# Layer 1 of a two-layer row attention: the softmax sums inverted once each and spread by transfers, and the seven block products added up on the way out of PSUM

## The chip, the cores and the metric

The kernel runs on one core of a Trainium2 chip. The metric is the time of one execution on the device in microseconds; the figure for a version is the median of its runs. TensorE is called PE, its weight load PEld, VectorE DVE, ScalarE ACT, GpSimd POOL, and SyncE, which issues the transfers, SP.

## The reference, cut to what matters

Two residual layers work on x of shape (1, 128, 256, 256): 128 rows of 256 tokens with 256 channels. Each begins with a group norm. Layer 0 is a gated attention with 8 heads and a pair bias; the change does not touch its arithmetic. Layer 1 is banded attention with 4 heads of 64 channels, in which a token sees the tokens up to 16 places away:

```
xn  = group_norm(x)
q, k, v = split(xn @ w_in.T + b_in)
s   = where(|i - j| <= 16, q k^T / sqrt(64), -inf)      per row and head
a   = softmax(s) v
out = x + a @ w_out.T + b_out
```

Everything is fp32.

## The kernel before, in words

Layer 0 walks through the 128 rows and leaves its output in DRAM as x1, channels on the partitions. Layer 1 reads that back in pairs of rows (`load1`, tile yg) and works in *rounds* of two rows. The order of the instructions on PE, ACT, DVE and POOL is the order of the program text, since `tc.manual_schedule` is on for these engines. SP is not in that list before; the scheduler places its transfers.

A round i, with s = 2i, runs these steps:

- `normal(i+2)` normalizes the pair i+2 on ACT (four activations, tile 1xn) and lets POOL make its four sums and differences (`row_sums`, tile 1ts).
- `scores(s)` and `scores(s+1)`: PE multiplies q and k in blocks of 64 keys by 96 queries, ACT takes the exponentials (1ex), POOL multiplies by the band's mask (1p) and adds two halves to 1zp, from which the softmax sums come.
- `attend(s-2)` and `attend(s-1)`: PE multiplies the weights 1p with the values into one half of the PSUM tile avz, and 1zp with a block of ones into the other half. The ones have 64 columns, so each softmax sum stands on the 64 partitions of its head, ready for a division by element.
- `total`: ACT copies the sums to SBUF (1z) and adds them up for a check at the end. `inverse`: DVE takes the reciprocal of 128x512 sums for each row. `divide`: DVE multiplies av by it, into 1at.
- `finish(i-3)`: DVE adds bias and residual to the output of pair i-3, turns it (`turn`, four transposes of 32x32 blocks) and stores it (`store`, four transfers of 128 KB).
- `row_sums` of 1at on DVE (tile 1att), `least` (DVE, minimum of the sums, for the check).
- `stretch(i+1, i-2)`: the three projections of 256 by 256 for a pair: q and k of pair i+1 and the output projection o of pair i-2.
- `values(s+2)` and `values(s+3)`: PE makes v in 64 matmuls (p1v), ACT copies it out.

A projection of a pair is done with seven products of 128x128 blocks in place of eight (class `Seven`). Each of the streams q, k and o has one PSUM bank with two halves. Product 2 goes to the upper half and is taken out at once[...]. Then the products follow each other into the two halves and accumulate there; after some of them ACT copies a half out (`take`). In the version before, all copies of the three streams are on ACT, and POOL adds the copies to the results afterwards (`add_two`, `add_mid`). `in_turn` issues the products of the three streams interleaved: 2 for each, (1, 5) for each, (3, 6) for each, 7 for each, 4 for each.

[...] Four form a ring (`proj_bank`, `sim_bank`) that scores, products and values use one after the other; four hold two avz tiles.

After the last round the two remaining pairs go through a tail without seven products (`project`, `add`, `turn_row`), and the check reads zmin and zsum; only if it fails, a slower path runs.

Of the kernel before, what the change touches and what calls it, by code (L numbers as in the profile page):

```python
# [9 lines left out]
F32 = mybir.dt.float32  # L10
AF = mybir.ActivationFunctionType
ALU = mybir.AluOpType
# [3 lines left out]
P = 128  # L16
# [23 lines left out]
def conv_preact_kernel(  # L40
# [142 lines left out]
    zmin = const.tile([P, 2 * S], F32, name="zmin")  # L183
    zsum = const.tile([P, 2 * S], F32, name="zsum")
# [387 lines left out]
    class Seven:  # L572


        def __init__(self, pool, weights, x, t, name, tag, by_token=False, bias=None, mid="mid"):
            self.weights, self.x, self.t, self.by_token, self.bias = weights, x, t, by_token, bias
            self.name, self.tag = name, tag
            self.to = pool.tile([P, 4, R], F32, tag=tag, name=name, bufs=2 if mid == "mid" else 1)

            self.mid = pool.tile([P, 2, R], F32, tag=mid, name=f"mid{name}", bufs=2 if mid == "mid" else 1)  # L580
# [19 lines left out]
        def copy(self, to, ps, half):  # L600

            if self.bias is None:
                nc.scalar.copy(to, ps)
            else:
                nc.scalar.activation(to, ps, AF.Identity, bias=self.bias[:, half : half + 1])

        def take(self, what):
            if what == "2":
                self.copy(self.two, self.ps[:, 1, :], 0)
            elif what == "15":  # L610
                nc.scalar.copy(self.to[:, 0:4:3, :], self.ps)
            elif what == "6":
                self.copy(self.mid[:, 0, :], self.ps[:, 0, :], 0)
            elif what == "7":
                self.copy(self.mid[:, 1, :], self.ps[:, 0, :], 1)
            elif self.bias is None:
                nc.scalar.copy(self.to[:, 1:3, :], self.ps)
            else:
                self.copy(self.to[:, 1, :], self.ps[:, 0, :], 1)
                nc.scalar.copy(self.to[:, 2, :], self.ps[:, 1, :])  # L620
# [39 lines left out]
    def in_turn(pool, sevens):  # L660

        for p in sevens:
            p.open()
            p.two = pool.tile([P, R], F32, tag=f"two{p.tag}", name=f"two{p.name}", bufs=1)

            p.product(2, p.ps[:, 1, :], first=True)
            p.take("2")
        for p in sevens:
            p.product(1)
            p.product(5)  # L670
            p.take("15")
        for p in sevens:
            p.product(3)
            p.product(6)
            p.take("6")
        for n, what in ((7, "7"), (4, "34")):
            for p in sevens:
                p.product(n)
                p.take(what)
        for p in sevens:  # L680
            p.add_two(p.two)
        for p in sevens:
            p.add_mid()
# [22 lines left out]
    with ExitStack() as both:  # L706
# [6 lines left out]
        ygs = {}  # L713

# [238 lines left out]
        with ExitStack() as lay:  # L953
# [6 lines left out]
            xns, tss, res = {}, {}, {}  # L960
# [30 lines left out]
            def stretch(i, j):  # L991


                streams = [
                    Seven(row, quarters1[w], xns[i], tss[i], f"1{w}{i}", w, bias=bqk[:, 0:2] if w == "q" else None,
                          mid=f"mid{w}")
                    for w in "qk"
                ]
                f, g = streams
                if j >= 0:  # L1000
                    outputs[j] = Seven(row, quarters1["o"], ats[j], ats_t[j], f"1o{j}", "out", mid="mido")
                    streams.append(outputs[j])
                in_turn(row, streams)
                for r in range(2):
                    st[2 * i + r].update(q=f.to[:, 2 * r : 2 * r + 2, :], k=g.to[:, 2 * r : 2 * r + 2, :])
# [50 lines left out]
            def attend(s):  # L1056
                if s < 0:
                    return
                (p, zp), v = hd.pop(s), st[s]["v"]

                avz = ps_av.tile([P, 2, 2, R], F32, tag="avz", name=f"1avz{s}", bufs=2)
                for b in range(NB):
                    for half in range(2):
                        for j in range(2):
                            keys, cols = slice(KB * half, KB * (half + 1)), slice(D1 * j, D1 * (j + 1))
                            q0, p0 = QLO[b], R * (b % 2) + QLO[b]

                            nc.tensor.matmul(
                                avz[cols, half, 0, q0 + QIN[b].start : q0 + QIN[b].stop],
                                lhsT=v[keys, b, cols],  # L1070
                                rhs=p[keys, j, p0 + QIN[b].start : p0 + QIN[b].stop],
                                start=(b == 0), stop=False,
                                skip_group_check=True,
                            )
                for half in range(2):
                    for j in range(2):
                        keys, cols = slice(KB * half, KB * (half + 1)), slice(D1 * j, D1 * (j + 1))
                        nc.tensor.matmul(
                            avz[cols, half, 1, :], lhsT=ones[keys, :], rhs=zp[keys, j, :],
                            start=False, stop=True,  # L1080
                            skip_group_check=True,
                        )
                hd[s] = avz

            def total(s):
                if s < 0:
                    return
                z = att.tile([P, 2, R], F32, tag="z", name=f"1z{s}", bufs=4)
                n = S + s
                nc.scalar.activation(z, hd[s][:, :, 1, :], AF.Identity, accum_out=zsum[:, n : n + 1])  # L1090
                st[s]["z"] = z

            def inverse(s):
                if s >= 0:
                    st[s]["rz"] = att.tile([P, 2, R], F32, tag="rz", name=f"1rz{s}")
                    nc.vector.reciprocal(st[s]["rz"], st[s]["z"])  # L1096

            def divide(s):
                if s < 0:
                    return  # L1100
                i, r = divmod(s, 2)
                if r == 0:
                    ats[i] = row.tile([P, 4, R], F32, tag="at", name=f"1at{i}", bufs=2)
                at = ats[i][:, 2 * r : 2 * r + 2, :]
                nc.vector.tensor_tensor(at, hd.pop(s)[:, :, 0, :], st[s]["rz"], ALU.mult)
                st[s]["at"] = at

            def least(s):
                if s >= 0:
                    n = S + s  # L1110
                    nc.vector.tensor_reduce(zmin[:, n : n + 1], st[s]["z"], axis=AX.XY, op=ALU.min)
# [43 lines left out]
            def finish(i):  # L1155
# [3 lines left out]
                ot = row.tile([P, 4, R], F32, tag="ot2", name=f"1ot2_{i}", bufs=1)  # L1159
                for half in range(2):  # L1160
                    nc.vector.scalar_tensor_tensor(
                        ot[:, half::2, :], outputs[i].to[:, half::2, :], bo_v[:, half : half + 1], ygs[i][:, :, half, :],
                        op0=ALU.add, op1=ALU.add,
                    )
                outputs.pop(i)
                for r in range(2):
                    st[2 * i + r]["ot"] = ot[:, 2 * r : 2 * r + 2, :]
# [5 lines left out]
            with tc.manual_schedule(engines={  # L1173
                mybir.EngineType.PE, mybir.EngineType.Activation, mybir.EngineType.DVE, mybir.EngineType.Pool
# [9 lines left out]
                for s in range(0, S + 2, 2):  # L1184
                    i = s // 2
                    bulk = s < S - 2
                    if bulk:
                        normal(i + 2, True)
                    if s < S:
                        scores(s)  # L1190
                        scores(s + 1)
                    attend(s - 2)
                    attend(s - 1)
                    total(s - 2)
                    total(s - 1)
                    if s < S:
                        finish(i - 3)
                    for r in (s - 2, s - 1):
                        inverse(r)
                        divide(r)  # L1200
                    if bulk:
                        if 0 <= i - 1 < S // 2 - 3:
                            ats_t[i - 1] = row.tile([P, 4, R], F32, tag="att", name=f"1att{i - 1}", bufs=2)
                            row_sums(ats_t[i - 1], ats[i - 1], nc.vector)
                        least(s - 2)
                        least(s - 1)
                        stretch(i + 1, i - 2)
                        values(s + 2)
                        values(s + 3)
                    else:  # L1210

# [3 lines left out]
                        add(s - 4, False)  # L1215
                        add(s - 3, False)
                for s in (S - 2, S - 1):
                    for _ in project(s):
                        pass
                add(S - 2, False)  # L1220
# [6 lines left out]

                for s in (S - 6, S - 5):
                    turn_row(s)
                add(S - 1, True)  # L1230
                for s in (S - 2, S - 4, S - 3):
                    turn_row(s)
                store(S - 1)
                for s in range(S - 4, S):
                    least(s)
# [198 lines left out]
```

## Time and profile before

| | |
|---|---|
| median of 3 runs | 3229.56 us (3226.58 to 3230.96) |
| profiled execution, time | 3227.81 us |
| profiled execution, span of the core | 3226.1 us |
| instructions | 87360 |
| busy over the span | PE 97%, PEld 75%, DVE 91%, ACT 65%, POOL 58% |
| granted TensorE clock, mean | 0.991 |
| layer 1 | from about 2086 us to the end |
| one round of layer 1 | 17.37 us |

The span lies within the execution's own time, which is what the medians count. "Busy" is recorded time in instructions. In a view of waits each line names an engine and line that stood still, and after the arrow the engine and line that ended the wait, then the time in total, how often, and the longest. In a timeline the first two numbers are start and duration in us; "x7" is how many instructions were merged; brackets hold the idle time before. In groups of instructions the last parts are busy time in us, mean ns of one, and idle time before. An fp32 product on PE is recorded as two matmuls.

### The profile page before, as it was taken

Reading aid. Unit: us, or ns where it says so; the run is one execution under the profiler, and the core shown is the slowest. Engines: PE = TensorE matmul, PEld = TensorE weight load, DVE = VectorE, ACT = ScalarE, POOL = GpSimd, SP = SyncE. Lnnn points to the kernel's source line nnn. Section 1 sums busy time; section 2 is a strip of 40 time slices with the busy share of each in tenths; the row PEclk is TensorE's granted clock in tenths of the full one; section 3 lists DMA queues with packets and bytes.
Section 4 is the critical chain, followed back from the end, with each engine's and each line's share of the span. In section 5 each row is a group of like instructions: output and inputs, shape, how many; then the busy total and the mean of one; then the engine's idle time right before and its main releaser. Section 6 shows DMA issues by size and latency. Waiting matters only on the chain.

```text
span 3226.1 us, 87360 instructions
## 1 busy us (share of the span) xinstructions
PE 3117.8 (97%) x36843; PEld 2435.0 (75%) x36843; DVE 2938.5 (91%) x3629; ACT 2105.2 (65%) x4621; POOL 1876.1 (58%) x1780
## 2 busy tenths in 40 slices
PE   7889999999999999999999999999999999999997
PEld 4567777777777777777777777678888888888886
DVE  4669999999999999999999999869999999999998
ACT  4656666666666666666666666477777777777774
POOL 3034444444444444444444444288999999999996
PEclk9989999999999999999999999999999999999998
DMA  9931111111111111111111111012222222222222
GB/s 382 423 93 46 54 41 40 41 34 38 36 41 34 40 34 41 34 41 34 41 34 41 34 41 34 28 28 67 55 67 56 66 67 54 67 67 54 67 59 44
DMA packets 346191, 209.40 MB, mean 65 GB/s; under 512 B 273592, under 2 KB 339136, under 8 KB 339648
## 3 DMA queue, kind: packets, MB, share of 16 engines
q1 hardware_dynamic: 344896, 201.37, 21.8%
q8 instruction: 292, 4.78, 0.6%
q0 software_dynamic: 752, 2.36, 0.2%
q14 instruction: 107, 0.88, 0.1%
q10 hardware_dynamic: 144, 0.00, 0.0%
HBM read 136.59 MB, written 67.11 MB: 63 GB/s over the span
## 4 chain that ended last, share of the span: by engine, by line
PE 82%; ACT 9%; DMA 5%; issue 2%; DVE 2%; POOL 0%; SPq 0%; DVEq 0%; ACTq 0%; POOLq 0%
PE sim L766 8%; PE p1v L1015 7%; PE po L691 7%; PE av L798 7%; PE bv L798 7%; PE p1q L594 6%; PE pv L598 6%; PE pq L594 6%; PE pk L594 5%; PE p1k L594 5%; PE pg L594 5%; PE p1o L594 5%; DMA pr<-in_L_conv_pair_repr_dram 4%; PE zs L812 4%; ACT 1ex L1044 3%; ACT 1xn L975 3%
## 5 line engine op out<-in xcount | busy, mean ns | idle before, releaser
L779 ACT ACTIVATE ex<-sim 128x512 f32<-128x512 f32 x1024 | 548.1, 606 | 431.5 <-PE sim L766 431.5
L788 DVE TENSOR_TENSOR both<-ex 128x512 f32<-128x512 f32 x512 | 483.7, 983 | 75.2 <-ACT ex L779 74.5
L1096 DVE RECIPROCAL 1rz<-1z 128x512 f32<-128x512 f32 x128 | 426.0, 3328 | 39.0 <-ACT 1z L1090 39.0
L828 DVE RECIPROCAL d<-d 128x512 f32<-128x512 f32 x128 | 429.2, 3353 | 4.4
L623 POOL TENSOR_TENSOR v<-v,twovg 128x256 f32<-128x256 f32 x64 | 75.0, 1173 | 548.3 <-ACT twovg L642 548.3
L766 PE MATMUL sim<-q,k 32*128 32x256 f32 x4096 | 295.7, 401 | 1.1 <-ACT ex L779 1.1
L691 PE MATMUL po<-at,out_sb 128*128 128x256 f32 x1024 | 285.1, 382 | 4.0 <-DVE at L846 4.0
L766 PEld LDWEIGHTS sim<-q,k 32*128 32x128 f32 x4096 | 186.4, 184 | 102.7 <-issue 95.1
L798 PE MATMUL bv<-bias_sb,v 128*32 128x256 f32 x4096 | 244.5, 379 | 0.7 <-DVE t L843 0.7
L798 PE MATMUL av<-ex,v 128*32 128x256 f32 x4096 | 244.5, 379 | 0.0
L1015 PEld LDWEIGHTS p1v<-w_in_t,1xn 128*64 128x64 f32 x4096 | 222.3, 137 | 21.6 <-PE p1k L594 20.2
L1015 PE MATMUL p1v<-w_in_t,1xn 128*64 128x128 f32 x4096 | 237.7, 274 | 0.3 <-DVE 1xn L977 0.3
L1046 POOL TENSOR_TENSOR 1p<-1ex,seen 128x768 f32<-128x768 f32 x128 | 232.5, 1817 | 2.6 <-ACT 1ex L1044 2.6
L623 POOL TENSOR_TENSOR q<-q,twoqk 128x256 f32<-128x256 f32 x64 | 47.3, 740 | 296.7 <-ACT twoqk L642 296.7
L691 PEld LDWEIGHTS po<-at,out_sb 128*128 128x128 f32 x1024 | 185.8, 192 | 25.3 <-issue 4.3
L798 PEld LDWEIGHTS bv<-bias_sb,v 128*32 128x32 f32 x4096 | 133.1, 110 | 88.8 <-issue 1.1
L798 PEld LDWEIGHTS av<-ex,v 128*32 128x32 f32 x4096 | 133.2, 110 | 87.8 <-issue 0.3
L748 DVE TENSOR_SCALAR xn<-xt,mean,rstd 128x256 f32<-128x256 f32 x256 | 180.0, 742 | 0.0
L1022 ACT COPY 1v<-p1v 128x512 f32<-128x512 f32 x128 | 75.0, 586 | 145.0 <-PE p1v L1015 145.0
L1053 POOL TENSOR_TENSOR 1zp<-1p 128x512 f32<-128x512 f32 x128 | 162.7, 1271 | 10.0
L333 DVE BATCH_NORM_STATS2 stats<-xs 128x6 f32<-128x128 f32 x512 | 100.3, 276 | 63.9 <-DMA xs<-in_x_dram 63.9
L827 DVE SCALAR_TENSOR_TENSOR d<-g,z 128x512 f32<-128x512 f32 x128 | 113.1, 884 | 40.7 <-ACT z L825 40.5
(290 smaller groups left out, 8541.0 us busy)
## 6 DMA issues: line engine op xcount, KB each, us to landing
pr<-in_L_conv_pair_repr_dram SPq DMA_DIRECT2D x32, 1024.0 KB, 23.1
xs<-in_x_dram SPq DMA_DIRECT2D x16, 2048.0 KB, 23.3
x<-o SPq DMA_DIRECT2D x64, 512.0 KB, 3.0
yg<-x SPq DMA_DIRECT2D x64, 512.0 KB, 3.9
out_dram<-1o SPq DMA_DIRECT2D x256, 128.0 KB, 3.4
xg<-in_x_dram SPq DMA_DIRECT2D x252, 128.0 KB, 3.1
qkv_sb<-in_L_conv_qkv_proj_dram POOLq DMA_DIRECT2D x4, 192.0 KB, 12.7
w_raw<-in_L_conv_w_in_dram POOLq DMA_DIRECT2D x1, 768.0 KB, 13.4
```

The source lines that it names most:

```text
L594: nc.tensor.matmul(out, lhsT=weights, rhs=moving, start=first, **flags)
L598: nc.tensor.matmul(out[:, cols], lhsT=moving[:, cols], rhs=weights, start=first and t2 == 0, **flags)
L691: nc.tensor.matmul(ps[:, m, :], lhsT=w[:, kt, m * P : (m + 1) * P], rhs=at[:, kt, :], start=(kt == 0), stop=(kt == 1),)
L748: nc.vector.tensor_scalar(xns[i][:, 2 * r + half, :], xt[:, half, :], mean0[:, half : half + 1], rstd0[:, half : half + 1], op0=ALU.subtra ...
L766: nc.tensor.matmul(sims[j][:, kt, :], lhsT=k[p0 : p0 + D0, 2 * r + half, kt * P : (kt + 1) * P], rhs=q[p0 : p0 + D0, 2 * r + half, :], sta ...
L779: nc.scalar.activation(ex[:, j], sims[j], AF.Exp, scale=1.0 / math.sqrt(D0))
L788: nc.vector.tensor_tensor(both[:, j : j + 2], ex[:, j : j + 2, 0, :], ex[:, j : j + 2, 1, :], ALU.add)
L798: nc.tensor.matmul(to[D0 * j : D0 * (j + 1), half, :], lhsT=v[:, 2 * r + half, c0 : c0 + D0], rhs=weights(4 * half + j, kt), start=(kt == ...
L828: nc.vector.reciprocal(d, d)
L1015: nc.tensor.matmul(ps[KB * half : KB * (half + 1), b, :], lhsT=xns[i][:, 2 * r + kt, KB * b : KB * (b + 1)], rhs=w_in_t[:, kt, 2 * C + P * ...
L1046: nc.gpsimd.tensor_tensor(p.rearrange("p j (r c) -> p (j r) c", c=WROW)[:, :, 0 : 2 * WSTEP] .rearrange("p r (t c) -> p r t c", c=WSTEP)[: ...
L1096: nc.vector.reciprocal(st[s]["rz"], st[s]["z"])
```

## The change

The change does four things in layer 1.

1. *The sums.* `attend` handles a pair at once. The av products of both rows go to one PSUM tile, 1av, and the sums to another, 1zs, with one buffer each. The block of ones is replaced by `place`, whose columns are ones for 16 partitions out of 64, so that the sums of both rows stand one beneath the other, 16 partitions each. `inverse` copies one half to SBUF (ACT), adds the other (DVE), takes the reciprocal of 128x256 (DVE), writes one partition of each sixteen to DRAM (rz_far, two transfers of 4 KB), and reads them back spread over 64 partitions each (near, two transfers of 256 KB). `divide` multiplies the whole pair by near. `bounds` does the work of `total` and `least` for the check on a pair.
2. *The products.* Class `Summed` takes every product out as it is made, in the order 2, 1, 5, 6, 7, 4, 3 for each of the three streams. Products 2, 5, 6 and 4 are copied out, for q and k by ACT, for o by DVE with bias and residual added; 1, 7 and 3 are added by DVE to what is there already. POOL's additions are gone, and so is the residual step of `finish`.
3. *Places.* `normal(i+2)` stands after `stretch`, `divide` after that, and the `row_sums` of 1at are on POOL. SP joins the engines whose order is the text's.
4. *The tail* is written for pairs.

The core of the diff:

```diff
-    def in_turn(pool, sevens):
+    class Summed(Seven):
...
+        def out(self, to, half, m, r):
+
+            ps = self.ps[:, half, :]
+            if self.y is not None:
+                nc.vector.scalar_tensor_tensor(
+                    to, ps, self.bias[:, m : m + 1], self.y[:, r, m], op0=ALU.add, op1=ALU.add
+                )
+            elif self.bias is None:
+                nc.scalar.copy(to, ps)
+            else:
+                nc.scalar.activation(to, ps, AF.Identity, bias=self.bias[:, m : m + 1])
+
+        def take(self, n):
+            to, ps = self.to, self.ps
+            if n == 2:
+                self.out(to[:, 0], 1, 0, 0)
+            elif n == 1:
+                nc.vector.tensor_tensor(to[:, 0], ps[:, 0, :], to[:, 0], ALU.add)
+            elif n == 5:
+                self.out(to[:, 3], 1, 1, 1)
+            elif n == 6:
+                self.out(self.mid, 0, 0, 1)
+            elif n == 7:
+                nc.vector.tensor_tensor(to[:, 3], ps[:, 0, :], to[:, 3], ALU.add)
+            elif n == 4:
+                self.out(to[:, 1], 0, 1, 0)
+            elif n == 3:
+                nc.vector.tensor_tensor(to[:, 2], ps[:, 1, :], self.mid, ALU.add)
+
+    def in_turn(sevens):
 
         for p in sevens:
             p.open()
-            p.two = pool.tile([P, R], F32, tag=f"two{p.tag}", name=f"two{p.name}", bufs=1)
 
             p.product(2, p.ps[:, 1, :], first=True)
-            p.take("2")
...
+            p.take(2)
+        for n in (1, 5, 6, 7, 4, 3):
             for p in sevens:
                 p.product(n)
-                p.take(what)
-        for p in sevens:
-            p.add_two(p.two)
-        for p in sevens:
-            p.add_mid()
+                p.take(n)
...
+            place = att.tile([P, 2, D1], F32, name="place", bufs=1)
+            nc.gpsimd.memset(place, 0.0)
+            for half in range(2):
+                for r in range(2):
+                    c = 32 * half + 16 * r
+                    nc.gpsimd.memset(place[KB * half : KB * (half + 1), r, c : c + 16], 1.0)
...
-            def attend(s):
-                if s < 0:
+            def attend(i):
...
+                av = ps_av.tile([P, 2, 2, R], F32, tag="av", name=f"1av{i}", bufs=1)
+                zs = ps_av.tile([P, 2, 2, R], F32, tag="zs", name=f"1zs{i}", bufs=1)
...
                             nc.tensor.matmul(
+                                zs[cols, half, 0, :], lhsT=place[keys, r, :], rhs=zp[keys, j, :],
+                                start=(r == 0), stop=(r == 1),
                                 skip_group_check=True,
                             )
...
+                zs = hd["av", i][1]
+                z = att.tile([P, R], F32, tag="z", name=f"1z{i}")
+                nc.scalar.copy(z, zs[:, 0, 0, :])
+                nc.vector.tensor_tensor(z, zs[:, 1, 0, :], z, ALU.add)
+                rz = att.tile([P, R], F32, tag="rz", name=f"1rz{i}")
+                nc.vector.reciprocal(rz, z)
+                for j in range(2):
+                    nc.sync.dma_start(
+                        out=rz_far[i % 2, j], in_=rz[D1 * j : D1 * (j + 1)].rearrange("(n c) q -> n c q", c=16)[:, 0, :]
+                    )
+                near = att.tile([P, 2, 2, R], F32, tag="near", name=f"1near{i}", bufs=1)
+                for j in range(2):
+                    nc.sync.dma_start(
+                        out=near[D1 * j : D1 * (j + 1)].rearrange("p h r q -> p (h r q)"),
+                        in_=rz_far[i % 2, j].rearrange("n q -> (n q)").partition_broadcast(D1),
+                    )
+                hd["z", i] = (z, near)
+
+            def divide(i):
+                if i < 0:
                     return
...
+                ats[i] = row.tile([P, 4, R], F32, tag="at", name=f"1at{i}", bufs=2)
+                nc.vector.tensor_tensor(
+                    ats[i].rearrange("p (r h) q -> p h r q", h=2), hd.pop(("av", i))[0], hd["z", i][1], ALU.mult
+                )
...
-                mybir.EngineType.PE, mybir.EngineType.Activation, mybir.EngineType.DVE, mybir.EngineType.Pool
+                mybir.EngineType.PE, mybir.EngineType.Activation, mybir.EngineType.DVE, mybir.EngineType.Pool,
+                mybir.EngineType.SP,
             }):
...
+                for i in range(S // 2):
+                    s = 2 * i
+                    bulk = i < S // 2 - 1
+                    scores(s)
+                    scores(s + 1)
+                    finish(i - 3)
+                    attend(i - 1)
+                    inverse(i - 1)
                     if bulk:
+                        stretch(i + 1, i - 2)
                         normal(i + 2, True)
...
+                        divide(i - 1)
                         if 0 <= i - 1 < S // 2 - 3:
                             ats_t[i - 1] = row.tile([P, 4, R], F32, tag="att", name=f"1att{i - 1}", bufs=2)
-                            row_sums(ats_t[i - 1], ats[i - 1], nc.vector)
...
+                            row_sums(ats_t[i - 1], ats[i - 1], nc.gpsimd)
+                        bounds(i - 1)
                         values(s + 2)
                         values(s + 3)
                     else:
-
                         for r in (s - 4, s - 3):
                             for _ in project(r):
                                 pass
...
+                            add(r, False)
+                        divide(i - 1)
+                last = S // 2 - 1
+                attend(last)
+                inverse(last)
...
+                divide(last)
+                for s in (S - 2, S - 1):
+                    for _ in project(s):
+                        pass
```

## The prediction

> **What bounds the kernel now.** I first read the page's busy shares and slices, to see where the edited stage lies and which engines are full in it.
>
> ```profile
> PE 3117.8 (97%) x36843; PEld 2435.0 (75%) x36843; DVE 2938.5 (91%) x3629; ACT 2105.2 (65%) x4621; POOL 1876.1 (58%) x1780
> ...
> PE   7889999999999999999999999999999999999997
> ...
> DVE  4669999999999999999999999869999999999998
> ...
> POOL 3034444444444444444444444288999999999996
> ```
>
> Layer 1 is the last third (POOL jumps from 4 to 8 or 9). It runs from 2086 us to the end, in 63 rounds of two rows. Next comes the busy time in a stretch well inside it.
>
> ```profile
> 2400.00:2800.00 400.00, 387.44 (x5754) 333.95 (x5753) 393.64 (x369) 289.33 (x691) 369.01 (x324) 1.00 0.25 63
> ```
>
> PE 97%, DVE 98%, POOL 92%: three engines look full, so the shares don't say which sets the round. The view of waits in 2400 to 3100 us (40 rounds) does:
>
> ```profile
> PEld p1q L594 <- ACT two1q L605: 37.9, 40, 1.0
> ...
> PE p1q L594 <- ACT two1q L605: 21.8, 40, 0.6
> PEld p1q L594 <- ACT 1ex L1044: 15.4, 40, 0.4
> ```
>
> PE waits twice in every round, and for ACT only; for DVE and POOL it never waits. PE is the bound, with two short stalls in each round behind ACT. The timeline of one round shows them:
>
> ```profile
> 2705.33 0.60 PE L1078 MATMUL 1avz<-1zp,ones 64*64 64x256 f32 x7
> ...
> 2705.87 0.70 PE L594 MATMUL p1q<-1xn,w_in_t 128*128 128x256 f32 x2
> ...
> 2707.42 0.50 ACT L605 ACTIVATE two1q<-p1q,bqk 128x256 f32<-128x256 f32 x1
> ...
> 2707.97 0.70 PE L594 MATMUL p1q<-1xn,w_in_t 128*128 128x256 f32 x2 [0.54 <-ACT two1q L605]
> ...
> 2708.51 0.59 PE L594 MATMUL p1q<-1ts,sums_1q 128*128 128x256 f32 x2
> ...
> 2708.94 0.59 PE L594 MATMUL p1k<-1xn,w_in_t 128*128 128x256 f32 x2
> ```
>
> Products follow each other every 0.4325 us (2708.51 to 2708.94), recorded 0.59 long, so an end lies 0.16 past the time at which PE is free. The last zs matmul ends at 2705.93, so PE is free at T = 2705.77. The values' first matmul stands at 2715.94 and a round lasts 17.37 us (2698.58 to 2715.94). From T to the values are 10.17 us for 21 products, that is 9.08: **1.09 us of each round are stalls**. Of them 0.21 lie ahead of the first product (ACT does the four 1xn before the exponentials, which free its bank), 0.81 ahead of product 1 of q, 0.07 at the values. A stalled product costs 0.11 beyond its wait, since its weights load unhidden (0.70 against 0.59).
>
> [...] DVE's L568 takes 1.38 us beside POOL's adds and L570 0.41 us alone. [...] the trace has 0.69 at 512, so 0.42 at 256 is my estimate. [...] the trace has no transfer as small as the new ones.
>
> **The change part by part.** *Off DVE:* two reciprocals 128x512, two divides, four subtractions, two reductions, two 1ot:
>
> ```profile
> L1096 DVE RECIPROCAL 1rz<-1z 128x512 f32<-128x512 f32 x81 | 269.2, 3324 | 0.0
> L1161 DVE SCALAR_TENSOR_TENSOR 1ot<-1o,bo_v,yg 128x512 f32<-128x512 f32 x80 | 84.9, 1100 | 0.0
> L569 DVE TENSOR_TENSOR 1att<-1at 128x256 f32<-128x256 f32 x40 | 59.8, 1494 | 0.0
> L1111 DVE TENSOR_REDUCE zmin<-1z 128x1 f32<-128x512 f32 x80 | 50.6, 672 | 0.0
> ```
>
> *On DVE now, per round:* transposes 1.41; the add of z 0.42; one reciprocal of 256 at 6.2 ns per element, 1.75 (0.17 for 2 elements, 3.34 for 512); nine sums out of PSUM at 0.42; four 128x256 out of PSUM with bias and y at 0.46 (L1129: 0.44 and 0.48); one divide of 1024, 1.22; one reduction 0.40. Sum 10.8, from 17.1. *ACT:* 2.08 normals, 1.6 exponentials, 1.17 values, 0.37 for z, 0.56 for its sum, 3.4 for eight takes: 9.2, from 12.6. *POOL* loses the adds (6.6) and gains four subtractions, 0.73 each[...]: 12.0, from 16.0. None of this is worth anything by itself, since PE waits for neither DVE nor POOL now.
>
> *PE's work* is the same: as many score, av, zs, product and value matmuls of the same shapes. Only its stalls can change. The 0.21 goes: the normals now follow the products on ACT, so the exponentials end about 2.6 us after the scores begin and the bank is needed 3.5 us after. The 0.81 goes too: ACT has only the short copy of z ahead of product 2 of q.
>
> **The new wait.** Every product now waits for the preceding take of its stream, and the o stream's takes are all on DVE. Its order is: add of z, reciprocal, take 2 of o. From T: zs ends 0.16; ACT starts 0.07 later (3191.41 to 3191.48 in the last round); copy 0.37 to 0.60; hand-over 0.04; add 0.42 to 1.06; 0.04; reciprocal 1.75 to 2.85; take 2 of o, which may start 0.08 earlier (as L843 behind L828), 0.46 to 3.23; hand-over 0.06; unhidden weights 0.11: **product 1 of o starts at 3.40**. It is due sixth, at 5 x 0.4325 = 2.16. Stall 1.24. Behind it in PE's queue stand 15 products, the values and the next scores. With the 0.07 at the values the round loses 1.31 against 1.09: **+0.22**, a round of 17.59. Bounds: 0.9 to 1.5 for the stall (-0.1 to +0.5), as the three 256-element durations are scaled.
>
> *Other takes:* matmul to take 0.63, DVE 0.42 to 0.46 or ACT 0.47, hand-over 0.06, weights 0.11: 1.22 to 1.27, against 3 x 0.4325 = 1.30 to the stream's next product. They just fit; I take 0, bounds 0 and +0.5 per round.
>
> *The transfers,* on SP, now in hand order: four stores (their transposes are over before T), two writes of 4 KB after the reciprocal, two broadcasts of 256 KB that wait for the writes, then the yg load. [...] the second issued 0.4 later; a broadcast at most 4.0 (yg, 512 KB): near lands about T+9.5, bounds 8 to 13. The divide stands behind the last take at T+11, ends at T+12.2, and frees av for the next attend at T+15.4. Cost 0; the cover is gone if near lands after T+14. POOL's subtractions then end near T+17 and the next round needs them at T+22; the masks behind them are needed at T+33.
>
> *Sum.* 60 full rounds x 0.22 = 13.2. The last full round had no normals before and took 16.58; it becomes 17.59: +1.0. The first two rounds have only q and k: steps of 1.22 against 0.865 there, but the scores no longer wait for POOL's adds (1.9): 0, bounds -2 and +3. *The end:* from the last T (3191.25) to the last DVE instruction (3218.69) were 27.4 us. Now av has one buffer: reciprocal 2.9, transfers 7, divide 1.2, attend 2.5 at the lower clock, again 2.9, 7 and 1.2, then eight products 4.1, the last takes, transposes and reductions 5.5: 34.3, so +7 (bounds +3 and +12). Total +21.2. The profiled execution took 3227.81 (span 3226.1), so 3249.0; the median shown lies 1.75 higher: **3251**.
>
> **The rivals.**
> 1. *Faster: ACT's stalls go and no other comes.* If take 2 of o were over at T+2.0, the round would be 17.37 - 1.02 = 16.35, and 61 x -1.02 + 7 gives 3174. For it: DVE sheds 6.3 us. Against it: that reciprocal can't begin before T+1.1. It decides where the stall falls below 0.87 (61 x -0.15 = -9, +7 from the end): 3227 and down. Chance 0.14, mostly near its edge.
> 2. *No change:* the stall is 0.9 to 1.0, so that the tail is about all that is left: 3229 to 3236. Chance 0.09. That the change isn't what it says is no rival: order and waits are written out by hand.
> 3. *The takes don't fit:* if DVE starts 0.73 after a matmul instead of 0.63, each step of o is 0.06 to 0.1 late, six times: +0.45 per round, 61 x 0.45 = 27 more: 3278. Chance 0.13.
> 4. *near is late:* landing at T+16, the divide holds av and each round grows by 2: 3370. The page gives the broadcast reads no precedent. Chance 0.06.
>
> **How the numbers follow.** The main case has 0.58, with 3238 to 3266 as its own range. About 0.2% (6.5 us) is what a measurement can tell from no change. Faster 0.14, same 0.09, slower 0.77. The range takes in rivals 2 and 3 and the edge of rival 1, and leaves out the full form of rival 1 and rival 4: 3222 to 3292.
>
> **What would show it.** Right: PE's product 1 of o waits for the DVE line of take 2 some 1.2 us in every round, PE's waits for ACT are gone, the round is 17.5 to 17.7, DVE near 61% busy, POOL near 68%. Wrong: a round under 17.2, PE waiting for L1135 (divide) through av, many small waits in the seven products, or the end less than 3 us longer.

## The result, and the profile after

The changed kernel takes **3252.5 us** in the median of 4 runs (3252.2 to 3255.7), the kernel before 3228.2 in 4 runs beside them: ratio 1.0077, 95% interval 1.0059 to 1.0094. It is slower by 0.8%, where 3251 was predicted. The profiled execution has a span of 3250.9 us, 24.8 more than before.

The busy times and slices of the page after, and the windows view of 2400 to 2800 us (the columns are the stretch, its length, then PE, PEld, DVE, ACT and POOL busy, the granted clock, the DMA share and GB/s):

```profile
PE 3121.9 (96%) x36843; PEld 2402.2 (74%) x36843; DVE 2523.8 (78%) x3946; ACT 1866.7 (57%) x4060; POOL 1610.4 (50%) x1651
...
DVE  4669999999999999999999999755655556556554
...
POOL 3044444444444444444444444266676666666763
```

```profile
2400.00:2800.00 400.00, 384.32 (x5651) 317.88 (x5653) 234.30 (x482) 199.01 (x477) 264.95 (x273) 1.00 0.40 92
```

DVE fell from 98% to 59% in this stretch, POOL from 92% to 66%, ACT from 72% to 50%. PE fell too, from 387.4 to 384.3 us of 400: the engine that sets the end waits a little longer than it did. A round went from 17.37 to 17.59 us. The waits view of 2400 to 3100 us says for whom:

```profile
PEld p1o L594 <- DVE 1o L662: 43.3, 40, 1.1
...
PE p1o L594 <- DVE 1o L662: 27.3, 40, 0.7
...
PEld p1q L594 <- issue: 15.0, 39, 0.4
```

The waits for ACT's `two1q` and `1ex` are gone, and one for DVE's take of o has come, in every one of the 40 rounds. The third line is as large as the old line for `1ex` (15.4) and has no releaser now; it comes back below. The timeline of one round, from the last sums on PE to the stalled product:

```profile
2713.98 0.60 PE L1102 MATMUL 1zs<-1zp,place 64*64 64x256 f32 x7
...
2714.51 0.70 PE L594 MATMUL p1q<-1xn,w_in_t 128*128 128x256 f32 x2
...
2714.64 0.37 ACT L1115 COPY 1z<-1zs 128x256 f32<-128x256 f32 x1 [0.86 <-PE 1zs L1102]
...
2715.05 0.42 DVE L1116 TENSOR_TENSOR 1z<-1zs,1z 128x256 f32<-128x256 f32 x1 [4.51 <-ACT 1z L1115]
...
2715.51 1.75 DVE L1118 RECIPROCAL 1rz<-1z 128x256 f32<-128x256 f32 x1
...
2717.18 0.39 DVE L662 SCALAR_TENSOR_TENSOR 1o<-p1o,bo_v,yg 128x256 f32<-128x256 f32 x1
...
2717.62 0.70 PE L594 MATMUL p1o<-1at,w_out_t 128*128 128x256 f32 x2 [0.68 <-DVE 1o L662]
```

Read it from below: product 1 of o starts when take 2 of o has left DVE, that take stands behind the reciprocal, the reciprocal behind the addition, and the addition behind ACT's copy of the sums. DVE had been idle for 4.51 us before the addition. An engine that is idle for 40% of the round still stops PE, because its 2.2 us of new work come exactly when its first take is due.

### The profile page after: what moved, and what is told of

Read it like the earlier page. It is cut to its first block, busy times and chain, and to the rows that moved or that the text cites. A ratio compares the mean times of both kernels' runs of the same rounds, so it can differ in the third digit from the quotient of the medians.

```text
span 3250.9 us, 87361 instructions
## 1 busy us (share of the span) xinstructions
PE 3121.9 (96%) x36843; PEld 2402.2 (74%) x36843; DVE 2523.8 (78%) x3946; ACT 1866.7 (57%) x4060; POOL 1610.4 (50%) x1651
## 3 DMA queue, kind: packets, MB, share of 16 engines
q0 software_dynamic: 752, 2.36, 0.2%
## 4 chain that ended last, share of the span: by engine, by line
PE 86%; DVE 7%; DMA 5%; ACT 1%; issue 1%; POOL 0%; SPq 0%; DVEq 0%; POOLq 0%; ACTq 0%
PE sim L781 8%; PE p1v L1036 7%; PE po L705 7%; PE av L813 7%; PE bv L813 7%; PE pv L598 6%; PE p1o L594 6%; PE pq L594 5%; PE pk L594 5%; PE pg L594 5%; PE p1q L594 4%; PE p1k L594 4%; PE zs L827 4%; DVE 1rz L1118 3%; PE 1sim L1057 3%; DMA pr<-in_L_conv_pair_repr_dram 3%
## 5 line engine op out<-in xcount | busy, mean ns | idle before, releaser
L668 ACT ACTIVATE 1q<-p1q,bqk 128x256 f32<-128x256 f32 x192 | 90.9, 473 | 308.5 <-PE p1q L594 308.4
L1116 DVE TENSOR_TENSOR 1z<-1zs,1z 128x256 f32<-128x256 f32 x64 | 27.2, 424 | 293.0 <-ACT 1z L1115 293.0
L568 POOL TENSOR_TENSOR 1ts<-1xn 128x256 f32<-128x256 f32 x64 | 47.0, 734 | 342.7 <-ACT 1xn L997 342.6
L662 DVE SCALAR_TENSOR_TENSOR 1o<-p1o,bo_v,yg 128x256 f32<-128x256 f32 x183 | 82.6, 451 | 106.6 <-PE p1o L594 106.6
```

## The experiments

**The reciprocal left out.** The sums themselves go to the transfers in its place, so the output is not normalized.

```
-                rz = att.tile([P, R], F32, tag="rz", name=f"1rz{i}")
-                nc.vector.reciprocal(rz, z)
+                rz = z
```

> The changed kernel without the reciprocal: the sums themselves, not their inverses, are written out and spread, so the output is wrong; all else stays. If product 1 of o waits only because the reciprocal stands ahead of take 2 of o on DVE (0.96 us of each round), take 2 begins when product 2 of o has ended, the stall goes, and the round is 16.63 instead of 17.59: 3252 - 61 x 0.96 = 3193. If instead the seven hand-overs through DVE pace the products, the round changes by under 0.3: 3234 or more. If the transfers hold av, they start 1.7 us earlier and the round falls by up to 1.7, but PE then shows its wait for the divide in the changed kernel, which it doesn't.

Measured: 3195.4 us in one run. The round is 16.64 us, 0.95 less than in the changed kernel, and PE was busy for 400.00 of the 400 us from 2400 to 2800. PE waits because of this one instruction: of its 1.75 us, 0.95 come back.

**The reciprocal in two halves, among the products.** The addition stays; 128 columns are inverted after the takes of product 1, the other 128 after those of product 5 (the transfers follow the second half).

```
-                nc.vector.reciprocal(rz, z)
+            def invert(i, half):
...
+                cols = slice(half * R // 2, (half + 1) * R // 2)
+                nc.vector.reciprocal(rz[:, cols], z[:, cols])
...
-                        stretch(i + 1, i - 2)
+                        stretch(i + 1, i - 2, {1: lambda: invert(i - 1, 0), 5: lambda: invert(i - 1, 1)})
```

> The whole computation: the reciprocal is cut into two of 128 columns (0.97 each from 0.17 for 2 and 1.75 for 256), the first issued on DVE after the takes of product 1, the second after the takes of product 5; the transfers follow it. If the reciprocal's place on DVE makes the stall, both halves fit into gaps between takes: product 1 of o is on time, 0.1 is left at later takes, round 16.7, 3252 - 61 x 0.87 = 3199. near then lands near T+12, the divide ends at T+13.7, still ahead of the next attend. If the transfers have no such slack, PE waits for the divide and the gain shrinks to nothing. If the hand-overs pace the products, it stays at 3240 or more.

Measured: 3202.0 us (3193.5 to 3202.4), ratio 0.9909, interval 0.9892 to 0.9925: the same work in another order is faster than both kernels. Its timeline:

```profile
2709.63 0.94 DVE L1128 RECIPROCAL 1rz<-1z 128x128 f32<-128x128 f32 x1
...
2710.59 0.48 DVE L662 SCALAR_TENSOR_TENSOR 1o<-p1o,bo_v,yg 128x256 f32<-128x256 f32 x1
...
2710.99 0.94 DVE L1128 RECIPROCAL 1rz<-1z 128x128 f32<-128x128 f32 x1
...
2718.71 1.23 DVE L1147 TENSOR_TENSOR 1at<-1av,1near 128x1024 f32<-128x1024 f32 x1 [2.43 <-DMA 1near<-rz_far]
```

Each half fits between two takes. The last line shows the price: the transfers now start so late that the divide waits for them. Most rounds are 16.64 us long, but more than a dozen are 16.7 to 17.4 (the mean of the first 29 is 16.76). In one of 17.00 the divide ended at 2334.69, and the weights of the next matmul into `av`, which has one buffer, began to load at 2334.81. That fits a wait for the divide, though the trace names no releaser there.

**The same place, not split.** Both halves stand one behind the other after the takes of product 1.

```
-                        stretch(i + 1, i - 2, {1: lambda: invert(i - 1, 0), 5: lambda: invert(i - 1, 1)})
+                        stretch(i + 1, i - 2, {1: lambda: (invert(i - 1, 0), invert(i - 1, 1))})
```

> The whole reciprocal (as two instructions of 128 columns, one right after the other, 1.76 us together) after the takes of product 1, where the halves had one of them each after product 1 and product 5. In the run of the halves the gap on DVE between those takes was 0.88 us and the next take of o ended 0.13 us before its buffer was wanted: a block of 1.76 us ends 0.8 us later there, so product 5 of o or the one after should wait 0.7 us in each round: 16.65 + 0.7 = 17.35, some 3202 + 61 * 0.7 = 3245. If the place alone mattered and not the size of the piece, it stays at 3202.

Measured: 3231.2 us in one run, rounds of 17.26 us. The 0.62 us more than a round of 16.64 are close to the 0.7 expected; the total is 14 below, since the halves' own mean round was 16.76 with its late transfers, and not 16.64. So the size of a piece counts as well as its place: DVE has gaps of about 0.9 us, and a piece of 1.75 (recorded) doesn't fit.

**The end alone.** The last pair's sums, reciprocal and transfers are issued ahead of the divide of the pair before it, and `near` gets a second buffer. Everything else is the changed kernel.

```
+                        last = S // 2 - 1
+                        sums(last)
+                        inverse(last)
                         divide(i - 1)
...
-                attend(last)
-                inverse(last)
+                attend(last, False)
```

> The changed kernel with another tail only: the sums of the last pair are multiplied before the divide of the pair ahead (near has two buffers), so that the two chains of copy, reciprocal and transfers overlap. The tail took 43.5 us from the last round's attend against 34.9 before. If the two transfer chains one after the other make that difference, the second (15 us from divide to divide) shrinks to about 5: 3252 - 9 = 3243. If the tail is bound by the products and stores at the end, under 3 us are gained. Rounds stay at 17.59.

Measured: 3242.9 us, ratio 1.0047, interval 1.0031 to 1.0064: 9.5 us below the changed kernel. The last divide starts at 3222.91 and not at 3231.86. Two trips through memory, one behind the other, were what made the end longer.

**Halves and end together.** 

> The two edits that each took time off, together: the reciprocal in two halves of 128 columns among the products, and the last pair's sums and transfers ahead of the divide of the pair before it. They lie in different stages, so their gains should add: 3202 (halves alone) less 9.5 (early sums alone against the change) gives 3192. Rival: the halves have already made the rounds so short that in the last round the transfers of the pair ahead are later than the products, and the early sums then take less than 5 us off: 3197 or more.

Measured: 3190.4 us (3185.7 to 3196.9), ratio 0.9887, interval 0.9871 to 0.9904: 11.6 below the halves alone, where the early sums took off 9.5 by themselves. The two gains add, within the spread of the runs. The edit is both diffs above, and nothing else.

**The kernel before, with the normalizing moved.** One call moves; no sum, product or take is touched.

```
-                    if bulk:
-                        normal(i + 2, True)
                     if s < S:
                         scores(s)
...
                         stretch(i + 1, i - 2)
+                        normal(i + 2, True)
```

> The kernel before with one thing of the change alone: the normalizing of the coming pair (four activations 1xn on ACT, four subtractions 1ts on POOL) issued after the stretch of products and not ahead of it. The prediction put 0.21 us at the head of the products and 0.81 us ahead of product 1 of q down to these activations. If so, both go and PE needs 16.35 us a round, and DVE with 17.09 us of work a round becomes the bound: 17.1 to 17.2 us a round, some 3212 to 3216. Second theory, after the trace of the changed kernel: the 0.2 us at the head is not ACT's and stays (its weight load shows 0.39 us of idle time without a releaser), only the 0.81 goes; the time is the same, since DVE bounds the round either way, and the trace of this run tells the two apart. Rival: the subtractions, issued later, fall beside DVE's sums and reciprocals and slow them, and the round stays at 17.4 or grows: 3228 to 3260.

Measured: **3185.8 us** (3183.1 to 3187.6), ratio 0.9868, interval 0.9852 to 0.9885, better than both theories and the fastest of all (the interval overlaps that of halves and end). The round is 16.61 us, and in the windows view (2400 to 2800 us) PE is busy throughout and POOL for 387 us in place of 369, while DVE stays at 98%:

```profile
sum 400.00, PE 400.00 PEld 348.32 DVE 393.37 ACT 313.84 POOL 387.08; mean PE 400.00 PEld 348.32 DVE 393.37 ACT 313.84 POOL 387.08
```

Waits of PE's weight loads in 2400 to 3100 us:

```profile
PEld p1q L594 <- ACT 1z L1090: 16.2, 42, 0.4
...
PEld p1q L594 <- ACT two1q L605: 6.9, 42, 0.2
```

What failed in the expectation is DVE as the next bound. Its 17.09 us a round weren't fixed: the same instructions take another time at another place in the round, beside other work of POOL.

```profile
2710.25 0.95 DVE L569 TENSOR_TENSOR 1att<-1at 128x256 f32<-128x256 f32 x1
...
2713.18 2.79 DVE L1161 SCALAR_TENSOR_TENSOR 1ot<-1o,bo_v,yg 128x512 f32<-128x512 f32 x2
```

Three of the four sums over rows took 1.4 to 1.5 us before, beside POOL's additions of 128x512, which took 1.46 to 1.49 there; now all four lie beside POOL's subtractions and take 0.65 to 0.95, and POOL's additions, away from them, 1.27. In an early round of the kernel before, the sum of L568 (from 2127.95) takes 1.38 us beside POOL's addition, and those of L569 and L570 right behind it 0.41 each, with POOL idle. The residual steps got slower in exchange, 2.79 us for the two where they took 2.11. On balance DVE's round has 16.34 us (393.37 / 400 * 16.61), just below PE's. The second theory was right about the head: 0.39 us of idle weight loads ahead of the first product are still there.

**The changed kernel, with the normalizing put back early.**

```
+                    if bulk:
+                        normal(i + 2, True)
                     scores(s)
...
                         stretch(i + 1, i - 2)
-                        normal(i + 2, True)
```

> The changed kernel with the normalizing of the coming pair put back where the kernel before had it, ahead of the scores (four activations 1xn on ACT, 2.08 us, and four subtractions 1ts on POOL). In the changed kernel's trace ACT has 1.44 us of idle time between the copies of the values and the copy of the sums (0.58 ahead of the exponentials, 0.86 ahead of the copy 1z), so 2.08 us more push the copy of the sums back by 0.65 us. The addition, the reciprocal and take 2 of o on DVE follow it, and the stall of product 1 of o grows from 0.96 to 1.6: 17.59 + 0.65 = 18.25 us a round, 3252 + 61 * 0.65 = 3292. Rival: the normalizing fits into ACT's idle time and only moves the exponentials: 3252.

Measured: 3276.7 us, ratio 1.0142, interval 1.0125 to 1.0159; rounds of 17.89 us. The direction is as expected, the size is half: 24 us and 0.30 a round, not 40 and 0.65. The waits view:

```profile
PEld p1o L594 <- DVE 1o L662: 54.1, 39, 1.4
```

The same wait has grown from 1.1 to 1.4 us. ACT's copy of the sums came 0.36 us after the last of them and not 0.06. The expectation took 1.44 us of idle time off the 2.08 and pushed the rest on; but ACT's recorded times overlap (the second copy of v is recorded until 2711.84, the first `1xn` from 2711.74), so the activations need less than the sum of their records.

**The sums part alone,** with the products, ACT's copies and POOL's additions of the kernel before, the sums over rows on DVE, and the residual ahead of the sums. Against the changed kernel:

```
-                    Summed(row, quarters1[w], xns[i], tss[i], f"1{w}{i}", w, bias=bqk[:, 0:2] if w == "q" else None)
+                    Seven(row, quarters1[w], xns[i], tss[i], f"1{w}{i}", w, bias=bqk[:, 0:2] if w == "q" else None,
+                          mid=f"mid{w}")
...
-                            row_sums(ats_t[i - 1], ats[i - 1], nc.gpsimd)
+                            row_sums(ats_t[i - 1], ats[i - 1], nc.vector)
```

> One part alone: sums inverted once and spread, with the order of the changed kernel, but the seven products as before (copies on ACT, additions on POOL, residual in finish, row_sums of 1at on DVE). No take is behind the reciprocal on DVE then. PE loses 0.20 at the head of the products and 0.07 at the values, ACT has only the copy of z ahead of take 2 of q: round 16.55, 3191. If POOL (15.7 us a round without contention) or its contention with DVE sets the round instead, 17.0 to 17.4: 3220 to 3245. If it is the spreading that costs the time and not the products' new takes, it is no faster than the changed kernel.

Measured: 3407.4 us, ratio 1.0554, interval 1.0536 to 1.0571. Both expectations missed by far. The timeline shows a loop through memory that neither had reckoned with:

```profile
2707.94 1.23 DVE L1123 TENSOR_TENSOR 1at<-1av,1near 128x1024 f32<-128x1024 f32 x1 [8.54 <-DMA 1near<-rz_far]
...
2709.22 0.84 PE L1080 MATMUL 1av<-1p,1v 64*64 64x80 f32 x32 [2.05 <-DVE 1at L1123]
...
2712.81 0.37 ACT L1103 COPY 1z<-1zs 128x256 f32<-128x256 f32 x1 [4.65 <-PE 1zs L1090]
...
2718.78 0.38 DVE L1104 TENSOR_TENSOR 1z<-1zs,1z 128x256 f32<-128x256 f32 x1
...
2728.53 1.23 DVE L1123 TENSOR_TENSOR 1at<-1av,1near 128x1024 f32<-128x1024 f32 x1 [7.58 <-DMA 1near<-rz_far]
```

Divide, values and sums, copy, 5.6 us until DVE reaches the addition, reciprocal, transfers, divide: 20.6 us around, and the next matmuls into `av` wait for the divide. The round shown takes 20.53 us. The first three full rounds still take 16.6, as expected; from then on the mean is 20.3 (18.8 to 21.8).

**The sums part alone, reordered.** The residual goes behind the reciprocal.

```
-                    finish(i - 3)
                     attend(i - 1)
                     inverse(i - 1)
+                    finish(i - 3)
```

> The sums part alone again, with the old products and additions, and the residual of the pair three back put after the reciprocal and not ahead of the sums on DVE. In the run of the sums alone the round of 20.53 us was a closed loop: divide 1.23, values and sums on PE 3.6, copy 0.37, then 5.6 us until DVE came to the addition of the two halves (behind four sums over rows of 1.4 to 2.0 and the residual with its transposes, 3.3 together), reciprocal 1.75, transfers to the next divide some 7.4. If that loop is the cause, taking 3.3 us out of it leaves 17.2 to 17.8 us a round, 3205 to 3240. If something else made that run slow (transfers that take longer beside the old products, or ACT), the round stays above 19 us: 3300 or more.

Measured: 3254.5 us, ratio 1.0077, interval 1.0060 to 1.0094, rounds of 17.62 us. One line moved takes off 153 us, 2.5 us a round in the mean (20.09 to 17.64 over the full rounds), so the loop was the cause. The time is 14 above the range, since another wait took its place:

```profile
PEld p1o L595 <- ACT 1o L612: 46.6, 40, 1.3
...
ACT 1o L612 <- DVE 1ot L1186: 43.8, 21, 2.2
```

ACT's copy of o now waits for the late residual (in 21 of the 40 rounds by this line), and PE for ACT. That the sums alone give the time of the whole change is a coincidence of two different stalls.

**The products part alone,** with the old two reciprocals of 512 columns and no transfers.

```
-                nc.vector.tensor_tensor(z, zs[:, 1, 0, :], z, ALU.add)
-                nc.vector.reciprocal(rz, z)
+                    st[s]["rz"] = att.tile([P, 2, R], F32, tag="rz", name=f"1rz{s}")
+                    nc.vector.reciprocal(st[s]["rz"], st[s]["z"])
```

> The products part alone: the takes on DVE and ACT, the places and POOL's sums as in the changed kernel, but the softmax sums as the kernel before made them (two reciprocals of 512 columns, 3.31 us each, on DVE, no transfers). Both reciprocals now stand on DVE between the sums and take 2 of o. The block that ended at 2717.18 in the changed kernel (0.42 + 1.75) becomes two of 3.31 from some 0.25 us later: it ends 4.8 us later, and product 1 of o waits that much longer: 17.59 + 4.8 = 22.4 us a round, 3252 + 61 * 4.8 = 3545, less some 10 for the last pairs' transfers that are gone: 3535. Rival: the queues of the products adapt (ACT and PE run ahead) and a round costs no more than DVE's own work of 16 to 17 us: 3230 to 3260.

Measured: 3629.8 us in one run, rounds of 23.89 us, 1.5 above the 22.4 expected.

```profile
2707.40 6.57 DVE L1117 RECIPROCAL 1rz<-1z 128x512 f32<-128x512 f32 x2 [2.87 <-ACT 1z L1111]
...
2714.32 1.22 PE L594 MATMUL p1o<-1at,w_out_t 128*128 128x256 f32 x2 [4.31 <-DVE 1o L662]
```

PE stands still for 4.31 us ahead of product 1 of o, where it was 0.68 in the changed kernel: 3.6 more and not 4.8. The sums of the two rows are copied one after the other here, so the first reciprocal starts earlier against the products than the expectation had it. What came on top, 2.7 us of the 6.3 a round, is seen in the windows view (granted clock third from the end):

```profile
2710.00:2714.00 4.00, 0.01 (x1) 0.00 (x0) 4.00 (x3) 0.00 (x0) 2.55 (x2) 0.88 0.20 70
2714.00:2716.00 2.00, 1.68 (x4) 1.41 (x5) 1.35 (x4) 0.00 (x0) 0.00 (x0) 0.50 0.00 0
...
2720.00:2722.00 2.00, 2.00 (x11) 1.64 (x10) 1.58 (x4) 0.22 (x1) 0.00 (x0) 1.00 0.00 0
```

After the pause PE ran at a granted clock of 0.50 for some 5 us. In this order the products need the sums part: the takes of o on DVE can't stand behind 6.6 us of reciprocals.

## Why the prediction was right, point by point

*What bounds the kernel: right.* PE set the round, with two short stalls. The kernel before with the normalizing late shows it from the other side: with DVE at 98%, PE's matmuls have no recorded wait left and its weight loads stand idle for 0.4 us at most, and 42 us are gone. DVE's lighter load was indeed worth nothing by itself.

*The 0.81 ahead of product 1 of q: right.* It was ACT's place. Moving one call in the kernel before took off 0.76 us a round.

*The 0.21 at the head: this step failed.* I put it down to ACT's exponentials behind the four `1xn`, and let it go. After the change the gap is still there:

```profile
2712.15 1.64 ACT L1065 ACTIVATE 1ex<-1sim 128x384 f32<-128x384 f32 x4 [0.58 <-POOL 1att L569]
...
2714.51 0.30 PEld L594 LDWEIGHTS p1q<-1xn,w_in_t 128*128 128x128 f32 x2 [0.39 <-issue]
```

The exponentials end at 2713.79, 0.7 us before the first product, and the weight loads are idle for 0.39 us all the same, 0.20 of it in PE's stream. The gap is there without the reciprocal, with the halves, and in the kernel before with the normalizing late, and its releaser reads `1ex`, `1z` or "issue" in turn. ACT isn't the cause. Whether the gap comes with the change from tiles of 64x64 to 128x128 or with the start of an accumulation was not tried and stays open. What the trace has speaks for the tiles: the first product of layer 1's first stretch (2089.51), which follows the values with their 128x64 tiles, has 0.17 us in place of 0.39, and product 1 of q (2715.91), which starts an accumulation too, has none.

*The 37.9 us ahead of product 1: the wait is there, its reason isn't shown.* In the kernel before, PE's weight loads for product 1 of q wait for ACT's `two1q`, the take of product 2 of q, in each of the 40 rounds; in the changed kernel those of product 1 of o wait for DVE's take in the same way (43.3 us). Why product 1 follows the take the traces don't tell.

*The stall of product 1 of o: right in kind, 0.95 us and not 1.24.* By the prediction's own count PE was free at T = 2714.42 (2713.98 and 0.60, less 0.16). Product 1 started effectively at 2717.73 (2717.62 and 0.11 for its weights), T+3.31 against 3.40. It was due later than I had it, since the head stayed: 0.20 + 5 x 0.4325 = T+2.36, not 2.16. The durations taken for 256 elements were good: reciprocal 1.75, addition 0.42, sums out of PSUM 0.42, take with bias 0.45 on the mean. The 0.42 doesn't follow from 0.69 at 512 alone; the trace before has 0.41 at 128x256 (L570). The 1.22 for the divide and the 0.40 for the reduction were the author's estimates; they took 1.22 and 0.41. POOL's subtractions took 0.73 each, as predicted.

*The other takes: 0 predicted, 0.10 measured,* 0.05 each at two products of o.

*The round.* 0.20 + 0.95 + 0.10 + 0.07 = 1.32, and the 10.39 us from T to the values at 2724.81 (2707.22 and a round) less 9.08 give 1.31. The 1.31 of the prediction was this very figure, out of other terms: the 0.20 at the head and the 0.10 of the other takes, which it put at nothing, make up for the 0.29 by which it took the stall too long. That they cancel is luck, and so is part of the closeness of 3251 to 3252.5. A right total doesn't prove its terms.

*near in time: right, out of two wrong terms.* DVE waits for no transfer in the rounds. In the end they take 6.5 us from the first write's issue (3210.25) to the divide (3216.75), T+9.4 where T+9.5 was predicted:

```profile
3216.75 1.23 DVE L1135 TENSOR_TENSOR 1at<-1av,1near 128x1024 f32<-128x1024 f32 x1 [6.52 <-DMA 1near<-rz_far]
...
3231.86 1.23 DVE L1135 TENSOR_TENSOR 1at<-1av,1near 128x1024 f32<-128x1024 f32 x1 [5.42 <-DMA 1near<-rz_far]
```

The first read waits for its write (SP by up to 0.5 us) and is issued 1.63 us after it (3211.88), so the write took no longer than that. The prediction's terms left some 2.25 us for it (T+9.5 less 2.85, 0.4 and 4.0), which was the author's estimate. From the first read's issue to the divide are 4.9 us, where the prediction allowed 4.0 for a broadcast. It is also not so that the trace before has no transfer as small: at its start lie three loads of 1 to 4 KB, which land after 12.0 to 12.2 us.

*The end: +7 predicted, +8.7 measured* (from the last T to the end of the span: 43.5 us against 34.9). The two waits above make it, and the run with early sums takes 9.5 off.

*The sum.* Up to the values of the second round +1.2 (predicted 0), from there to the last values +14.9 (14.2), end +8.7 (7): 24.8 us of span against 21.2.

*The rivals.* Rival 1 (no other stall, 3174) has its run in the kernel without the reciprocal: 3195, in rounds of 16.64. That is its 16.35, in which the 0.07 at the values is counted already, with the head (0.20) and the other takes (0.10) added. Rival 3 (takes that don't fit) is there with 0.10 a round in place of 0.45. Rival 4 (near late) doesn't happen in the change, but it begins with the halves, and in the sums alone it set the round.

*What the change consists of.* With the normalizing late, the kernel before takes 3185.8 and the changed kernel 3252.5; with it early, 3228 and 3276.7. So one moved call brings the change 24 us (42 in the kernel before), and sums and products, with their order, cost 48 to 67, 9.5 of it in the end. Of the parts tried apart, only the one that looks like housekeeping gained time. And with both repairs, the halves and the early sums, the change (3190.4) isn't shown to beat the kernel before with that one call moved (3185.8).

## What to carry to other kernels

When three engines are 92 to 98% busy, read the waits of the one that sets the end: here the cure was to move eight instructions, not to remove 40% of another engine's work. Work on an engine with time to spare still costs time if it stands ahead of something that the bound engine needs at once, here 0.95 us for a reciprocal of 1.75; cut it to the size of the gaps, here pieces of 0.94 us in gaps of about 0.9. And where a result goes out to memory and back into the same round's loop, add up the whole loop, including what stands ahead of each step in its queue.

## What the runs showed of the hardware

A pause of PE cost more than its length in the products alone. With 0.68 us of recorded idle time a round ahead of product 1 of o (the changed kernel) and with 0.99 (normalizing early) the granted clock is 1.00 over the stretch from 2400 to 2800 us. With 4.31 us (the products alone) it is 0.85 over that stretch. In the round shown it is 0.50 from 3 us after PE stopped, from 2713.0 to 2719.8 us by the windows view; PE works for 5.5 of these 6.8 us, a product comes every 0.85 us and not every 0.43, and that adds 2.7 us to the pause.

Shorter pauses were followed by 0.50 as well. In the sums alone PE stands still for 2.05 us ahead of `av` in the round shown, and the granted clock is 0.78 from 2709 to 2711 us, 0.50 from 2711 to 2713 and 1.00 from 2715 on; from 2400 to 2800 us it is 0.95. At the end of the kernel before a pause of 2.79 us lies ahead of the last `av`, and the clock is 0.50 from 3199 to 3202 us. No run here changes the length or the place of a pause alone, so what decides is not shown.

DVE's share of busy time wasn't a measure of its work: the same sums over rows took up to 1.50 us beside POOL's additions and 0.65 to 0.95 at another place in the round, and the two residual steps went the other way, from 2.11 to 2.79 us. A DVE at 98% still gave way by 0.75 us a round.
